# Windowed attention inside an image kernel: 21 passes of three score units instead of 28 of two or three

## The chip, the cores and the metric

The kernel runs on one core of one Trainium2 chip. The metric is the device time of one execution in microseconds. Before the change it is 4560.12 us, the median of three runs (4557.74 to 4571.01).

The core has a matrix engine (PE), a vector engine (DVE), an engine for activations (ACT), a general one (POOL) and one that issues most of the transfers (SP). Each runs its own queue in order; semaphores tie them together. Matrix products land in PSUM[...]; every other tile named here is in SBUF. All data is 32-bit float, and each matmul leaves two records in the trace.

## The reference, cut to what matters

The input is 32 images of 128 channels and 64 x 64 pixels. Each image passes a dynamic 3 x 3 convolution and is then read as 4096 tokens of 128 channels. The tokens are normalised, projected to 16 channels and cut into 55 windows of 144 tokens with a stride of 72, and attention of 4 heads of 4 channels runs inside each window:

```python
win = jnp.transpose(xb[:, idx, :], (0, 1, 3, 2))
flat = win.reshape(Bc * num_w, WIN, D)
qkv = flat @ in_proj_w.T + in_proj_b
...
scores = jnp.einsum('nhqd,nhkd->nhqk', q, k) / np.float32(np.sqrt(HD))
attn = jax.nn.softmax(scores, axis=-1)
o = jnp.einsum('nhqk,nhkd->nhqd', attn, v).transpose(0, 2, 1, 3).reshape(Bc * num_w, WIN, D)
o = o @ out_proj_w.T + out_proj_b
...
recon = jnp.zeros((Bc, Tc, D), xb.dtype).at[:, flat_idx, :].add(o)
```

The result is projected back, added, normalised, and goes through a product with W and a batch norm. A recurrence `y = sigmoid(wx + y @ V.T)` over the 4096 tokens of all images ends the kernel.

## The kernel before, in words

The program has an image stage and, from about 4020 us on, the recurrence (`by_runs`), which has lines of its own and is not touched. It also builds slower branches for other inputs (`images_by_shift`, `by_steps`), which don't run here.

**Who sets the order.** The image stage is a set of Python generators, one for each job and image: `load`, `taps`, `waves`, `conv`, `drain`, `project`, `feed`, `values`, `attend`, `divide0`, `divide1`, `tail`, `last`, and one `setup`. Each yields the engine that its next step needs and the tiles that the step reads and writes. A planner, `Clock`, keeps an account of when each engine and tile is free by a table of costs (`cost`). It takes the step that can start first; between steps that could start at the same time a due time from the table `DUE` decides. A step that yields a fifth value, True, is preferred among these. So the order on each engine is fixed when the program is built, and several images are under way at once. Costs and due times change this order and nothing else. Since every engine is recorded by one helper, all instructions of the stage stand under L242 in the profile; they are told apart by their tiles.

In `cost` a PE step has one of three modes: full (128 x 128 weights), row (32 rows of the array in use, so that four matmuls run side by side on four groups of rows) and col (32 columns, four side by side). A change of mode is charged 0.11.

**Attention of one image.** The windows of an image are handled in `NWG` = 7 blocks `m`, each with `u` = 0 and 1. Four groups of rows `q` work side by side.

- `feed` makes the queries `qs`, the keys `ks`, the last 16 keys of each window spread over eight groups (`kt`), and the values: `Vc` for the first 128 keys and `VT` for the last 16.
- `values` makes for each `s` = 2m + u the masked queries `qe`: POOL multiplies `qs` by the head mask, [128, 4 heads, 144]. Then ACT copies the values into `VE`. There are two buffers of `qe` and of `VE`.
- `attend` runs 14 sets `s` with two passes `hp` each. A pass makes the scores of two heads: four matmuls in row mode with 288 columns each, into the only score tile `sc` (four banks, one for each row group). In the first pass of each block (u = 0, hp = 0) four more matmuls with 144 columns add the scores of the last 16 keys. ACT takes the exponentials of the two heads into `ex` and, in the first pass of a block, those of the extra keys into `ext`, in a second instruction. Then the scores of the next pass may be written. The weighted sums (col mode, 144 columns each) of the pass before follow its scores on PE, into the bank `av`: eight matmuls a pass, and four more with `ext` in each hp = 0. Between passes the planner puts other work of PE, such as the convolution's matmuls with 512 columns (`nm<-u,w`, `nm<-u,h`).
- The bank `av` holds up to three sets (432 columns). DVE copies it to `avs` after the sets 2, 5, 7, 10 and 13. A new group of sets begins with a wait for that copy.
- `divide` divides in two halves (blocks 0 to 3 and 4 to 6) by the sums of the exponentials: transfers to `cd`, a reciprocal, a way through DRAM, a product in `avs`, then a projection in row mode, `sc<-avs,wc`, which uses the same score tile and which DVE adds to `zt`.

Of the kernel before, what the change touches and what calls it, by code (L numbers as in the profile page):

```python
# [8 lines left out]
F32 = mybir.dt.float32  # L9
# [4 lines left out]
P = 128  # L14
# [6 lines left out]
NH = 4  # L21
# [20 lines left out]
    "setup": (0.2, 0.2, 8),  # L42
    "load": (-0.91, 0.63, 29),
    "taps": (0.2, 0.11, 6),
    "waves": (-0.12, 0.52, 26),
    "conv": (-0.43, 1.01, 36),
# [3 lines left out]
    "values": (1.27, 1.15, 28),  # L50
    "attend": (1.24, 1.1, 89),
    "divide0": (1.92, 0.12, 15),
# [6 lines left out]
class Clock:  # L59
# [115 lines left out]
    def cost(self, eng, op, out, ins):  # L175
        n = max(self.width(a) for a in (out, *ins))
        if eng == "PE":
# [7 lines left out]
            if mode != self.mode:  # L185
                c += 0.11
# [71 lines left out]
def hybrid_kernel(  # L258
# [57 lines left out]
    cen = const.tile([P, P], F32, name="cen")  # L316
    nc.vector.tensor_scalar_add(cen, ident, -1.0 / P)
# [36 lines left out]
    bdr = const.tile([P, DK], F32, name="bdr")  # L354
    nc.scalar.dma_start(bdr, b_down.partition_broadcast(P))
    ipr = const.tile([P, 3 * DK], F32, name="ipr")
    nc.scalar.dma_start(ipr, in_proj_b.partition_broadcast(P))
    ipT = const.tile([DK, 3 * DK], F32, name="ipT")
    nc.scalar.dma_start(ipT, in_projT)
    okf = const.tile([P, 1], F32, name="okf")  # L360
    oki = const.tile([P, 1], mybir.dt.int32, name="oki")
    with tc.tile_pool(name="sb1", bufs=1) as sb1, tc.tile_pool(
        name="ps1", bufs=1, space=bass.MemoryType.PSUM
    ) as ps1:
        one_ = sb1.tile([P, P], F32, name="one_")
# [53 lines left out]
    def images(nc):  # L419
# [6 lines left out]
        with ExitStack() as pa:  # L426
# [161 lines left out]
            def load(b):  # L588
# [61 lines left out]
                pl = one.tile([P, P], F32, name="pl")  # L650
# [21 lines left out]
                h = two.tile([P, 9 * P], F32, name="h")  # L672
# [245 lines left out]
            def feed(b):  # L918

                for m0, m1 in ((0, 3), (3, 6), (6, NWG)):  # L920
                    while ("gt", b) not in done or (
                        b and (gone.get(("att", b - 1), 0) <= 4 * m1 if m1 < NWG else ("sets", b - 1) not in done)
                    ):
                        yield
# [61 lines left out]
            exk = kept([P, 2, 4, 2, WIN], "ex")  # L986
            exl = kept([P, 4, WIN], "ext")
            qes = [kept([P, NH, WIN], f"qe{i}") for i in range(2)]

            def values(b):  # L990

                for s in range(2 * NWG):
                    m, u = s // 2, s % 2
                    while ("fed", b, m // 3 * 3) not in done or (
                        gone.get(("att", b), 0) < 2 * s - 1 if s else b and ("sets", b - 1) not in done
                    ):
                        yield
                    o = m * WIN
                    v0 = VEs[s % 2]
                    qe = qes[s % 2]  # L1000
# [7 lines left out]
                    )  # L1008
                    yield "ACT", None, (Vc[:, P * m : P * (m + 1)],), (v0,)
# [8 lines left out]
            def attend(b):  # L1018
# [5 lines left out]
                zt = done["gt", b][0]  # L1024

                def weighted(s, ap, hp, ex, ext):

                    m, u = s // 2, s % 2
                    c0, c1 = group(s)
                    o = slice(WIN * (s - c0), WIN * (s - c0 + 1))  # L1030
                    for h in range(2):
                        for q in range(4):
                            v = NR * (NH * q + 2 * hp + h)
                            nc.tensor.matmul(
                                ap[32 * q : 32 * q + 32, o],
                                VEs[s % 2][:, v : v + 32],
                                ex[:, q, h, :],
                                start=(hp == 0 and h == 0),
                                stop=(hp == 1 and h == 1),
                            )  # L1040
                    if hp == 0:
                        for q in range(4):
                            v = NR * (NQ * m + 2 * q + u)
                            nc.tensor.matmul(
                                ap[32 * q : 32 * q + 32, o],
                                VTf[:, v : v + 32],
                                ext[:, q, :],
                                start=False,
                                stop=False,
                            )  # L1050
                    elif s == c1 - 1:
                        copies.append((av[:, WIN * c0 : WIN * c1], ap[:, 0 : WIN * (c1 - c0)]))

                def group(s):
                    return next(g for g in ((0, 3), (3, 6), (6, 8), (8, 11), (11, 14)) if g[0] <= s < g[1])

                held, copies = None, []
                ap = avp
                exs, ext = exk, exl
                for s in range(2 * NWG):  # L1060
                    m, u = s // 2, s % 2
                    while (b and s == 10 and ("div", b - 1, 1) not in done) or gone.get(("values", b), 0) <= s:
                        yield
                    o = m * WIN
                    qe = qes[s % 2]
                    for hp in range(2):
                        yield "PE", scs, (qe[:, 2 * hp : 2 * hp + 2, :], ks[:, o : o + P], qs[:, o : o + WIN])
                        ps = clock.take("PE", scs)
                        for q in range(4):
                            r = slice(32 * q, 32 * q + 32)  # L1070
                            nc.tensor.matmul(
                                ps[:, q, 0 : 2 * WIN],
                                ks[r, o : o + P],
                                qe[r, 2 * hp : 2 * hp + 2, :],
                                start=True,
                                stop=True,
                            )
# [1064 lines left out]
```

## Time and profile before

| what | value |
|---|---|
| median of 3 runs | 4560.12 us |
| the profiled execution | 4565.91 us |
| its span, first to last instruction | 4564.1 us |
| granted PE clock over the span | 0.968 |
| PE idle before score matmuls (`sc<-qe,ks`) | 103.0 us |
| PE busy in a stretch of 124 us in the middle (2000 to 2124 us) | 120.24 us |

The profile page gives for each engine the busy time and its share of the span. Its groups list, for one kind of instruction, the total and the mean of one, and behind the bar the idle time that the engine had just before these, with what ended it. The waits list who waited for whom, in total microseconds, number of times and the longest. The timeline gives the start, the length and the number of records of merged instructions. A matmul's end is modelled, so that a group's length there can overlap the start of the next; the distance between starts does not.

### The profile page before, as it was taken

What the parts mean: (1) busy time and instruction counts of PE and PEld (TensorE: products, weight loads), DVE (VectorE), ACT (ScalarE), POOL (GpSimd) and SP (SyncE); (2) the same over time, 40 slices, a digit from 0 to 9 for tenths busy, and PEclk for the clock granted to TensorE, in tenths of its full rate; (3) what the DMA queues carried; (4) which work ended last, traced back from release to release, by engine and by line L of the source; (5) the groups of instructions that cost most, each with busy time, mean ns of one, the idle gap of its engine ahead of it and who ended that gap; (6) DMA issues with size and microseconds to landing.
All of it is one profiled execution on the core that took longest, in us unless ns stands there. A gap on an engine that the chain in (4) does not pass through costs nothing. (4 is left out here: it accounts for less than half of the span.)

```text
span 4564.1 us, 102113 instructions
## 1 busy us (share of the span) xinstructions
PE 4165.5 (91%) x41515; PEld 2074.1 (45%) x41515; DVE 3511.6 (77%) x5300; ACT 2465.8 (54%) x3948; POOL 1648.9 (36%) x1652
## 2 busy tenths in 40 slices
PE   5999999999999999999999999999999998589987
PEld 2444444444444444444444444444444444245543
DVE  7778878787787788778787877888778854459884
ACT  1455555545555555555555555555555555357774
POOL 3333333333333333324233333333333412027765
PEclk9999999999999999999999999999999998789998
DMA  3435545454654555555554555455456444459998
GB/s 100 130 108 164 180 158 186 158 174 143 188 179 155 177 177 167 179 162 172 167 185 154 168 176 159 167 179 173 159 163 200 140 168 167 158 222 240 278 268 174
DMA packets 467573, 789.36 MB, mean 173 GB/s; under 512 B 338048, under 2 KB 348304, under 8 KB 434320
## 3 DMA queue, kind: packets, MB, share of 16 engines
q1 hardware_dynamic: 456480, 715.38, 47.4%
q0 software_dynamic: 8704, 67.11, 7.2%
q8 instruction: 332, 5.44, 0.5%
q14 instruction: 153, 1.25, 0.1%
q10 hardware_dynamic: 1904, 0.18, 0.0%
HBM read 499.06 MB, written 276.76 MB: 170 GB/s over the span
## 5 line engine op out<-in xcount | busy, mean ns | idle before, releaser
L242 ACT ACTIVATE ex<-sc 128x1152 f32<-128x1152 f32 x896 | 1013.2, 1131 | 841.7 <-PE sc L242 806.6
L242 POOL TENSOR_TENSOR qe<-qs,mqk 128x576 f32<-128x576 f32 x448 | 605.4, 1354 | 747.5 <-PE sc L242 742.1
L242 PE MATMUL nm<-u,w 128*128 128x512 f32 x1536 | 796.1, 629 | 17.9 <-POOL w L242 16.0
L242 PE MATMUL sc<-qe,ks 32*128 32x288 f32 x7168 | 699.8, 460 | 103.0 <-ACT ext L242 42.4
L242 PE MATMUL av<-ex,VE 128*32 128x144 f32 x14336 | 631.4, 294 | 20.0 <-DVE avs L242 19.9
L242 PEld LDWEIGHTS sc<-qe,ks 32*128 32x128 f32 x7168 | 285.8, 185 | 619.1 <-issue 175.7
L242 PEld LDWEIGHTS av<-ex,VE 128*32 128x32 f32 x14336 | 371.7, 110 | 349.7 <-issue 255.6
L1972 PE MATMUL v<-yw,fVT 128*128 128x254 f32 (+1 forms) x1504 | 436.9, 428 | 34.8 <-ACT yw L1985 25.0
L242 POOL TENSOR_TENSOR u<-frames 128x528 f32<-128x528 f32 x256 | 380.3, 1493 | 185.3 <-PE nm L242 182.7
L1983 ACT ACTIVATE yw<-v,shf 128x254 f32<-128x254 f32 (+1 forms) x752 | 354.6, 474 | 120.6 <-DVE v L1978 48.3
L1978 DVE SCALAR_TENSOR_TENSOR v<-zr,scl,v 128x256 f32<-128x256 f32 (+1 forms) x585 | 347.2, 665 | 90.3 <-PE v L1972 89.8
L242 PE MATMUL nm<-u,h 128*128 128x512 f32 x768 | 397.7, 626 | 3.5 <-DVE frames L242 3.5
L242 PEld LDWEIGHTS nm<-u,w 128*128 128x128 f32 x1536 | 257.3, 191 | 287.6 <-issue 254.4
L1972 PEld LDWEIGHTS v<-yw,fVT 128*128 128x128 f32 x1504 | 241.7, 194 | 243.6 <-ACT yw L1983 194.1
L242 ACT ACTIVATE place<-zt 128x1024 f32<-128x1024 f32 x256 | 262.9, 1053 | 84.8 <-DVE zt L242 66.8
L242 PE MATMUL nm<-zt,fWc 128*128 128x512 f32 x512 | 291.4, 666 | 7.8 <-ACT zt L242 6.9
L1989 POOL COPY zr<-yw 128x256 f32<-128x256 f32 x416 | 256.8, 730 | 85.7 <-ACT yw L1983 85.4
L242 DVE SCALAR_TENSOR_TENSOR u<-u,u 128x528 f32<-128x528 f32 x256 | 244.0, 966 | 49.1 <-POOL u L242 47.6
L242 ACT COPY zt<-nm 128x512 f32<-128x512 f32 x256 | 149.7, 586 | 203.3 <-PE nm L242 197.0
L242 PE MATMUL nm<-place,avg 128*32 128x256 f32 x3072 | 238.3, 391 | 13.5 <-ACT place L242 13.1
L242 POOL TENSOR_TENSOR kt<-ks,mqk 128x384 f32<-128x384 f32 (+1 forms) x96 | 78.3, 815 | 426.2 <-ACT ks L242 381.4
L242 DVE SCALAR_TENSOR_TENSOR zt<-sc,gbk,zt 128x576 f32<-128x576 f32 (+1 forms) x192 | 174.9, 911 | 71.1 <-PE sc L242 70.3
(204 smaller groups left out, 6178.2 us busy)
## 6 DMA issues: line engine op xcount, KB each, us to landing
place<-r_d SPq DMA_DIRECT2D x384, 512.0 KB
place<-in_conv_k_dram SPq DMA_DIRECT2D x128, 576.0 KB
x_d<-frames SPq DMA_DIRECT2D x32, 2112.0 KB
place<-x_d SPq DMA_DIRECT2D x128, 528.0 KB
frames<-in_x_dram SPq DMA_DIRECT2D x128, 512.0 KB
out_dram<-zt SPq DMA_DIRECT2D x64, 1024.0 KB
z_d<-zt SPq DMA_DIRECT2D x64, 1024.0 KB
zr<-z_d SPq DMA_DIRECT2D x26, 2048.0 KB
```

Source lines behind the costliest of these rows:

```text
L242: got = f(*args, **kw)
L1972: nc.tensor.matmul(self.ps[:, :, c], fVT, self.yw[1 - r % 2][:, :, c], start=not whole, stop=True)
L1978: nc.vector.scalar_tensor_tensor(v, z, scl, v, ALU.mult, ALU.add)
L1983: nc.scalar.activation(y[:, :, c], self.ps[:, :, c], AF.Sigmoid, bias=shf)
L1989: nc.gpsimd.tensor_copy(z, y)
```

## The change

Score units are regrouped. A block has nine units of 144 columns: four heads for u = 0, the last 16 keys, and four heads for u = 1. Before, they were made in four passes of 3, 2, 2 and 2 units; after, in three passes of three units each. The middle pass has head 3 of u = 0, the last keys and head 0 of u = 1; these have different weights or queries, so it takes three groups of four matmuls with 144 columns, where the other two passes take four matmuls with 432 columns. One exponential instruction takes all three units. The tile `ex` becomes two tiles of three units, used in turn; `ext` is gone. The weighted sums of a block go to 288 columns of `av`, and DVE copies them to `avs` once a block, seven times an image.

`values` sets a mark of its own behind the queries, and the copy to `VE` waits for a later step of `attend`. `attend` waits for both marks. Gates that count passes are adapted (`feed`).

To make room in SBUF, `cen`, `bdr`, `ipr`, `ipT` and `rep` move into pools or tiles that are free at that time, `pl` becomes a part of `h`, and `cd` has one buffer instead of two. In the planner, leaving full mode is charged 0.19 instead of 0.11, and some due times differ.

```diff
 DUE = {
-    "setup": (0.2, 0.2, 8),
+    "setup": (0.27, 0.02, 8),
...
-    "taps": (0.2, 0.11, 6),
+    "taps": (-0.14, 0.29, 6),
...
-    "conv": (-0.43, 1.01, 36),
+    "conv": (-0.45, 1.09, 36),
...
-    "values": (1.27, 1.15, 28),
-    "attend": (1.24, 1.1, 89),
-    "divide0": (1.92, 0.12, 15),
+    "values": (1.44, 1.24, 28),
+    "attend": (1.24, 1.1, 71),
+    "divide0": (1.88, 0.1, 15),
...
             if mode != self.mode:
-                c += 0.11
+                c += 0.19 if self.mode == "full" else 0.11
...
-                pl = one.tile([P, P], F32, name="pl")
+                h = two.tile([P, 9 * P], F32, name="h")
+                pl = h[:, 0:P]
...
-            exk = kept([P, 2, 4, 2, WIN], "ex")
-            exl = kept([P, 4, WIN], "ext")
+            exs = [kept([P, 4, 3, WIN], f"ex{i}") for i in range(2)]
...
-                        gone.get(("att", b), 0) < 2 * s - 1 if s else b and ("sets", b - 1) not in done
+                        gone.get(("att", b), 0) < 3 * m - 1 + u if m else b and ("sets", b - 1) not in done
...
+                    gone["queries", b] = s + 1
+                    while gone.get(("att", b), 0) < 3 * m + u:
+                        yield
                     yield "ACT", None, (Vc[:, P * m : P * (m + 1)],), (v0,)
...
+                def scores(m, j, ps):
+
+                    o = m * WIN
+                    keys = ks[:, o : o + P]
+                    if j == 1:
+                        units = (keys, qes[0][:, 3]), (kt[:, m], qs[:, o : o + WIN]), (keys, qes[1][:, 0])
+                    else:
+                        units = ((keys, qes[j // 2][:, j // 2 : j // 2 + 3]),)
+                    w = 3 * WIN // len(units)
+                    for i, (k, q) in enumerate(units):
+                        for g in range(4):
+                            r = slice(32 * g, 32 * g + 32)
+                            nc.tensor.matmul(ps[:, g, w * i : w * i + w], k[r], q[r], start=True, stop=True)
+
+                def weighted(m, j, ex):
+
+                    for i in range(3):
+                        if j == 1 and i == 1:
+                            values_of(m, 1, 0, 0, ex[:, :, 1], False, True)
+                        else:
+                            n = 3 * j + i - (3 * j + i > 4)
+                            values_of(m, 0, n // 4, n % 4, ex[:, :, i], n % 4 == 0, n == 7)
+                    if j == 1:
+                        values_of(m, 1, 1, 0, ex[:, :, 1], False, False)
+
+                def values_of(m, extra, u, h, ex, first, last):
+
+                    for g in range(4):
+                        v = NR * (NQ * m + 2 * g + u) if extra else NR * (NH * g + h)
+                        t = VTf if extra else VEs[u]
+                        nc.tensor.matmul(
+                            ap[32 * g : 32 * g + 32, WIN * u : WIN * (u + 1)],
+                            t[:, v : v + 32],
+                            ex[:, g],
+                            start=first,
+                            stop=last,
+                        )
...
-                for s in range(2 * NWG):
-                    m, u = s // 2, s % 2
-                    while (b and s == 10 and ("div", b - 1, 1) not in done) or gone.get(("values", b), 0) <= s:
+                for p in range(3 * NWG):
+                    m, j = p // 3, p % 3
+                    while (
+                        (b and m == 5 and ("div", b - 1, 1) not in done)
+                        or gone.get(("queries", b), 0) <= 2 * m + (j > 0)
+                        or gone.get(("values", b), 0) < 2 * m + j
+                    ):
                         yield
...
+                    scores(m, j, ps)
+                    if held is not None:
+                        if held[1] == 0:
+                            yield "PE", None, (held[2],), (ap,)
+                        else:
+                            yield "PE", None, (held[2],)
+                        weighted(*held)
+                        if held[1] == 2:
+                            copies.append((av[:, 2 * WIN * (m - 1) : 2 * WIN * m], ap[:, 0 : 2 * WIN]))
+                    gone["att", b] = p + 1
+                    ex = exs[(b + p) % 2]
+                    yield "ACT", None, (ps,), (ex,), True
+                    nc.scalar.activation(
+                        ex.rearrange("p q h t -> p q (h t)"), ps[:, :, 0 : 3 * WIN], AF.Exp, scale=HD**-0.5
+                    )
...
-                cdt = two.tile([P, WIN], F32, name="cd")
+                cdt = one.tile([P, WIN], F32, name="cd")
```

## The prediction

> **What bounds it now.** I read the page's busy table first, then the busy time by stretch, to see which engine fills the stage that the change touches; then the waits of that engine, and its timeline, to price it. The busy table of the page:
>
> ```profile
> PE 4165.5 (91%) x41515; PEld 2074.1 (45%) x41515; DVE 3511.6 (77%) x5300; ACT 2465.8 (54%) x3948; POOL 1648.9 (36%) x1652
> ```
>
> Busy time by stretch (columns: length, PE, weight loads, DVE, ACT, POOL, granted clock, DMA share, GB/s):
>
> ```profile
> 1000.00:2000.00 1000.00, 951.46 (x10382) 465.67 (x10380) 791.59 (x1167) 544.23 (x825) 337.30 (x280) 0.98 0.52 167
> 2000.00:3000.00 1000.00, 956.10 (x10458) 468.05 (x10452) 807.59 (x1165) 543.26 (x819) 338.70 (x280) 0.98 0.54 173
> 4020.00:4564.00 544.00, 477.35 (x1620) 264.86 (x1620) 403.19 (x730) 367.64 (x769) 338.22 (x544) 0.94 0.88 240
> ```
>
> The image stage runs to about 4005 us; there PE is busy 95 to 96% of the time and the next engine, DVE, 80%. The last row is the recurrence, which the change leaves alone. The chain that ended last lies wholly in the recurrence, so it doesn't help here: in the image stage PE itself is the chain, and each microsecond taken from PE's order is one off the end, as long as no wait grows.
>
> What it costs PE to do a pass is in its timeline (start, length, group; the 2 records of each matmul are counted in x). I use the distance from one start to the next, because ends are modelled:
>
> ```profile
> 2004.84 0.77 PE L242 MATMUL sc<-qe,ks 32*128 32x288 f32 x8
> 2005.54 0.70 PE L242 MATMUL av<-ex,VE 128*32 128x144 f32 x16
> 2006.06 0.43 PE L242 MATMUL av<-ext,VT 128*32 128x144 f32 x8
> 2006.41 1.13 PE L242 MATMUL nm<-u,w 128*128 128x512 f32 x2
> 2007.47 0.77 PE L242 MATMUL sc<-qe,ks 32*128 32x288 f32 x8
> 2008.06 0.42 PE L242 MATMUL sc<-qs,kt 32*128 32x144 f32 x8
> 2008.41 0.70 PE L242 MATMUL av<-ex,VE 128*32 128x144 f32 x16
> 2009.04 1.99 PE L242 MATMUL nm<-u,w 128*128 128x512 f32 x4
> 2010.95 0.77 PE L242 MATMUL sc<-qe,ks 32*128 32x288 f32 x8
> ...
> 1110.10 1.01 PE L242 MATMUL sc<-avs,wc 17*128 17x432 f32 x8
> 1111.04 1.98 PE L242 MATMUL nm<-u,w 128*128 128x512 f32 x4
> ```
>
> *Full tiles* (128*128): one matmul takes 1.06 to the next start (2006.41 to 2007.47), two take 1.91: 0.86 each and **0.20 a visit**. *Row tiles* (32*128 and 17*128, four side by side): 288 columns take 0.70, 432 take 0.94; so 144 columns cost 0.24, which the extra keys (kt) repeat (0.59 + 0.35 against 0.70), and 0.22 remains **a visit**. *Column tiles* (128*32): 8 matmuls take 0.63 to a full one, and four more, those of VT, lengthen this by 0.24, so streaming is 0.49 and **a visit 0.14**. These steps repeat to a few ns all over the image stage.
>
> **Part 1: 21 passes instead of 28.** Nothing is taken from the work itself: 4,480 score matmuls and 8,960 weighted ones in both kernels, and 9,072 score columns an image in both (28 x 288 + 7 x 144; 21 x 432). What goes are visits. I counted them in the PE order of both built programs, image stage: row tiles are entered 1,078 times before and 840 after, column tiles 1,103 and 928, full tiles 1,043 and 960. So 238 x 0.22 + 175 x 0.14 + 83 x 0.20 = 52 + 24 + 17 = **93 us**. The middle score group of a pass is now three groups of 144 columns; the first of them after a visit begins has no row, but kt's second half follows its first without any extra, so I take 0.22 for it as well (at worst the gain on 224 such passes is 0.1 us less each, 22 us; it could not be better by more than the same). At the granted clock of 0.98 the 93 become 95.
>
> A rule of the Trainium skill speaks against this: TensorEngine Tiling (Array Packing), Performance Considerations, puts the overhead on each matmul, some 60 cycles, whatever its width. By that, with the number of matmuls the same, the change saves nothing: 0 us, and 4560. The row decides against it: four more matmuls in the same mode cost 0.24, which is their columns, and what is left over comes once a visit. The same page says, without a figure, that a change of tiling mode drains TensorE; the visit's 0.14 to 0.22 is what that drain and refill cost here.
>
> **Part 2: the wait for the exponentials.** There is one score tile, so each pass's scores wait for the exponentials of the pass before, and PE must have other work meanwhile. PE's waits:
>
> ```profile
> PE sc L242 <- ACT ext L242: 46.0, 43, 3.0
> PE sc L242 <- ACT ex L242: 35.2, 63, 3.0
> PE av L242 <- DVE avs L242: 19.9, 11, 4.8
> PE sc L242 <- POOL qe L242: 17.0, 24, 3.7
> ```
>
> The rows of ACT and of the copies:
>
> ```profile
> L242 ACT ACTIVATE ex<-sc 128x1152 f32<-128x1152 f32 x896 | 1013.2, 1131 | 841.7 <-PE sc L242 806.6 <-DVE cp L242 19.3 <-DVE bnmv L242 8.6
> L242 ACT ACTIVATE ext<-sc 128x576 f32<-128x576 f32 x224 | 144.5, 645 | 0.0
> L242 DVE COPY avs<-av 128x432 f32<-128x432 f32 x128 | 77.0, 601 | 93.8 <-PE av L242 93.1
> L242 DVE COPY avs<-av 128x288 f32<-128x288 f32 x32 | 14.4, 451 | 33.9 <-PE av L242 33.9
> ```
>
> From 576 and 1152 elements (645 and 1131 ns) a start of 159 ns and 0.844 ns an element: 1728 elements take 1.62 us. From the start of its scores to the earliest next scores a plain pass needs 0.70 + 0.20 (ACT's start behind the scores, 2005.74 in the trace) + 1.13 + 0.06 = about 2.1 us; the pass with the extra keys 0.94 + 0.20 + 1.13 + 0.65 = about 2.85 (two exponentials); every pass after, 0.94 + 0.20 + 1.62 + 0.06 = 2.8. So the longest wait is not longer, while every pass brings 12 or 16 weighted matmuls instead of 8 or 12 to fill it. Before, the pass with the extra keys had 0.94 + 0.63 of its own and lacked 1.3 us, more than one 512-column matmul's 1.06; after, each has 0.94 + 0.87 or more and lacks at most 1.0, which one such matmul covers. I then walked the PE order of both programs with the steps above and summed what falls short between two passes: before, 133 passes lack 84 us (the trace has 46.0 + 35.2 on ACT and part of 17.0 on POOL, so the walk can be trusted); after, 94 passes lack 49. That is **35 us** less. ACT's work falls from 1,158 to 672 x 1.62 = 1,087 us, unseen at 54% busy.
>
> **Part 3: copies per block.** Five copies an image become seven of 288 columns: from 128 x 0.601 + 32 x 0.451 = 91 to 224 x 0.451 = 101 us of DVE, hidden behind PE. The weighted matmuls of a new block wait for the copy, with at least the next scores and a filler (0.94 + 1.06) in between, where before it was 0.70 + about 0.8. So the 19.9 us may rise with 224 chances for 160 (+8) or go (-20); I take 0. SBUF moves (cen, cd, pl, the small loads) and the setup's due times act once, or reuse a tile whose last reader is a whole phase past; no DMA is added, SP's transfers are the same in number. 0 us, up to 10 either way. The query multiplies on POOL (1.35 us each) get two whole passes' time, about 4.6 us; before, about 3.5. The copy into VE now waits for a step of attend of its own. In the built order of ACT it stands between the exponentials of two passes, so the later ones are queued behind it, and behind these PE's next scores; but there ACT waits for PE anyway (806.6 us of idle in the row of ex), and the copy is 0.24 us: nothing, or at worst its 448 x 0.24 x the share of passes that are short (94 of 672), 15 us, which the 10 to 35 below take in.
>
> **Part 4: due times and a dearer tile change** only reorder; their visits and lacks are already in the counts. What is late next is DVE: 98.7 us an image of some 123 before (its mean over six stretches of one image each), of some 119 after, 83%. PE already waits for DVE 39.3 us at the divided outputs and 20 at the convolution's; I charge 10 us more (0 to 35).
>
> **Sum.** -95 - 35 + 10 = -120 on the profiled execution of 4565.9 (span 4564.1 and 1.8 around it): 4446. That run lies 5.8 above the median, so 4560 - 120 = **4440**.
>
> **Rivals.** (a) *Given back*: the visits go, but DVE and the order around it take up the slack, as PE's waits for ACT don't shrink and those for DVE grow by 35: -95 + 35 = -60, 4500. For it: DVE at 80% and in order; against: the walk's fit to the waits of before. (b) *More*: all the avs wait and most of the ACT wait go, and fewer holes keep the clock up (0.98 in the middle, 3,780 x 0.02 = 75 us lost, a third back): -95 - 60 - 20 - 5 = -180, 4380. (c) *Slower*: ACT is in order, and a copy of 0.59 us (nm to zt) or 0.24 (VE) that stands before the exponentials delays the only score tile; with 1.62 us to follow, the filler then falls short. It decides from 130 / 672 = 0.19 us a pass upward; at 0.25 a pass, 168 us, the time is 4600. Against: only 94 passes are short by count. The same page of the skill, under PSUM Bottleneck, warns that emptying PSUM becomes the limit after tiling, and wants two engines for it; here ACT alone does it, yet 21 x 2.8 = 59 us an image is half of the period, so by the trace it doesn't bind. (d) That it doesn't do what it says: the order shows 672 passes of 1728 elements; nothing is left for it but chance.
>
> **How the numbers follow.** Forecast 0.60 (own range 4410 to 4470); (a) 0.25; (b) 0.09; (c) 0.04; (d), or no change, 0.02. The range reaches to (a)'s 4500 less a little and below the forecast's end, since the widest sums of the unknowns are -50 and -165: 4402 to 4492. A change under 0.3% can't be told from none here. Faster 0.94, same 0.02, slower 0.04.
>
> **What would show it.** PE busy in the image stage down by some 95 us with idle lower by about 30; score groups of 432 columns at 0.94 to the next start; the middle group near 0.95; ACT's row for 1728 elements at 1.62; waits of sc for ACT near 50 us. It is wrong if the middle group costs over 1.05, if the waits for ACT pass 100, or if those for DVE grow by more than 35.

## The result, and the profile after

The changed kernel takes **4505.22 us**, the median of four runs (4492.03 to 4507.87); the kernel before, in four runs on the same chip, takes 4565.57. The ratio is 0.9861 (95% interval 0.9831 to 0.9891). The change makes the kernel faster by 1.4%, half of the forecast 120 us; 4505 lies 13 us above the range of 4402 to 4492.

The profiled execution takes 4507.87 us, its span is 4506.1, and the clock granted over it 0.958 (0.968 before). First the busy table of the page after, one line:

```profile
PE 4099.9 (91%) x41515; PEld 2055.8 (46%) x41515; DVE 3562.1 (79%) x5364; ACT 2407.2 (53%) x3500; POOL 1680.8 (37%) x1652
```

Then the busy time by stretch (columns: length, PE, weight loads, DVE, ACT, POOL, granted clock, DMA share, GB/s):

```profile
1000.00:2000.00 1000.00, 956.30 (x10650) 471.45 (x10648) 834.26 (x1199) 535.23 (x712) 354.74 (x285) 0.97 0.55 174
2000.00:3000.00 1000.00, 946.33 (x10524) 468.95 (x10522) 835.74 (x1212) 539.67 (x727) 356.11 (x291) 0.97 0.54 172
3962.00:4506.00 544.00, 478.27 (x1620) 264.76 (x1618) 401.64 (x723) 366.00 (x769) 338.60 (x544) 0.94 0.88 239
```

The recurrence (last row) is what it was. In the image stage more matmul records fit in 1000 us, but PE isn't less idle, and the clock fell from 0.98 to 0.97. The steps that were priced beforehand are all there. The timeline of two passes after (start, length, group; the last one is cut short):

```profile
955.67 0.53 PE L242 MATMUL sc<-qe,ks 32*128 32x144 f32 x8
956.02 0.42 PE L242 MATMUL sc<-qs,kt 32*128 32x144 f32 x8
956.26 0.42 PE L242 MATMUL sc<-qe,ks 32*128 32x144 f32 x8
956.62 0.94 PE L242 MATMUL av<-ex,VE 128*32 128x144 f32 x24
957.49 0.38 PE L242 MATMUL nm<-cv,grp 128*128 128x1 f32 x2
...
959.29 1.01 PE L242 MATMUL sc<-qe,ks 32*128 32x432 f32 x8
960.23 0.45 PE L242 MATMUL av<-ex,VE 128*32 128x144 f32 x8
```

A score group of 432 columns takes 0.94 to the next start, the middle group 0.35 + 0.24 + 0.36 = 0.95, twelve weighted matmuls 0.87. So do the rows of the exponentials and of the copies (1611 ns against 1.62 forecast, 100.6 us against 101):

```profile
L242 ACT ACTIVATE ex<-sc 128x1728 f32<-128x1728 f32 x672 | 1082.5, 1611 | 869.0 <-PE sc L242 854.6 <-DVE u L242 7.0 <-PE av L242 5.2
L242 DVE COPY avs<-av 128x288 f32<-128x288 f32 x224 | 100.6, 449 | 190.7 <-PE av L242 189.6
```

What is different is whom PE waits for. The waits after:

```profile
PE sc L242 <- DVE zt L242: 90.2, 47, 4.7
PE nm L242 <- DVE h L242: 52.6, 20, 3.5
PE sc L242 <- ACT ex L242: 28.2, 54, 1.2
...
PE sc L242 <- ACT VE L242: 12.2, 17, 0.8
PE sc L242 <- DVE avs L242: 10.6, 8, 5.6
...
PE sc L242 <- POOL qe L242: 2.6, 1, 2.6
PE av L242 <- DVE avs L242: 2.0, 4, 0.7
```

and before, the two that grew (the scaled plane had a tile of its own, `pl`):

```profile
PE sc L242 <- DVE zt L242: 39.3, 27, 4.8
...
PE nm L242 <- DVE pl L242: 18.0, 8, 2.9
```

The wait for the exponentials of the extra keys (46.0) is gone, that for `ex` fell from 35.2 to 28.2, for `qe` from 17.0 to 2.6, for the copies into `avs` from 19.9 to 2.0. In their place PE waits for DVE: 51 us more where it waits for `zt`, 35 more where the logits product (`nm<-fcwT`) waits for the scaled plane.

I then added up, over the image stage (from the span's start to the first matmul of the recurrence), PE's idle time by the engine that released it, and the time that the clock took away (half of every period granted at half speed). "Work" is the count of PE's visits and columns in the built order, priced as in the prediction; what is left over in the sum is 13 us before and -6 after, so sums of this kind are good to some 20 us.

| image stage, us | before | after | difference |
|---|---|---|---|
| end of the stage | 4021.6 | 3961.5 | -60 |
| PE's work by count | 3563 | 3471 | -92 |
| lost to the half-speed clock | 112 | 156 | +44 |
| PE idle | 333 | 340 | +7 |
| of it for DVE | 170 | 231 | +61 |
| for ACT | 121 | 74 | -48 |
| for POOL | 34 | 28 | -6 |

The visits came as counted. The missing 60 us are idle time that did not fall by 25 but rose by 7, and a clock that was taken as given and lost 44. Together these are 76; the other 16 lie within what the sum leaves over.

**The first new hole.** The timeline after, around one logits product (the brackets give the idle time before and who ended it; only the lines of three engines that matter are kept):

```profile
961.10 1.31 POOL L242 TENSOR_TENSOR kt<-ks,mqk 128x384 f32<-128x384 f32 x1
...
961.63 0.79 DVE L242 TENSOR_TENSOR gl<-gr 128x1 f32<-128x1 f32 x1
...
962.36 1.30 POOL L242 TENSOR_TENSOR u<-frames 128x528 f32<-128x528 f32 x1
962.45 1.23 DVE L242 SCALAR_TENSOR_TENSOR gl<-gv,gl 128x1 f32<-128x1 f32 x1
963.63 1.14 POOL L242 TENSOR_TENSOR qe<-qs,mqk 128x576 f32<-128x576 f32 x1
963.72 0.15 DVE L242 TENSOR_SCALAR gl<-gl 128x1 f32<-128x1 f32 x1
963.90 0.88 DVE L242 TENSOR_TENSOR gr<-gr,gl 128x1 f32<-128x1 f32 x1
...
965.26 0.36 PE L242 MATMUL nm<-fcwT,h 128*128 128x4 f32 x2 [2.97 <-DVE h L242]
...
966.48 1.82 PE L242 MATMUL sc<-qe,ks 32*128 32x432 f32 x8
```

Three steps on a single column take 0.79, 1.23 and 0.88 us; each ends where the GpSimd product beside it ends (962.41, 963.66, 964.77). The step at 963.72, which has only one input in SBUF, takes 0.15 beside the same product. PE waits 2.97 us for the chain, of which the three steps have 2.4 from standing beside GpSimd, and the scores that follow are 1.82 long where those at 959.29 are 1.01: the clock has dropped to half. DVE is not idle before the step that writes the scaled plane, in either trace, so the plane's move into `h` isn't what delays it. Of the 96 such two-input steps (32 images, three each) 31 took more than 0.25 us before and 57 after, and every one of these ended within 0.2 us of the end of a GpSimd instruction. The tile's own rows (shortest/median/longest ns) before:

```profile
L242 DVE TENSOR_TENSOR gl<-gr x32: 147/160/1283, 28.5 to 3582.0; 128x1 f32<-128x1 f32 x32
L242 DVE SCALAR_TENSOR_TENSOR gl<-gv,gl x32: 159/160/1280, 28.7 to 3583.4; 128x1 f32<-128x1 f32 x32
```

and after:

```profile
L242 DVE TENSOR_TENSOR gl<-gr x32: 147/491/1148, 28.8 to 3548.7; 128x1 f32<-128x1 f32 x32
L242 DVE SCALAR_TENSOR_TENSOR gl<-gv,gl x32: 158/1165/1253, 29.0 to 3549.5; 128x1 f32<-128x1 f32 x32
```

The Trainium skill has the rule behind it (SBUF — State Buffer, Who interferes with whom): a DVE instruction with both inputs in SBUF and a GpSimd instruction that reads SBUF exclude each other for the whole instruction. The rows agree, for steps of a single column too. The kernel's planner counts this exclusion only for steps wider than one column, so it places these chains as if GpSimd were not there.

**The second.** The timeline after, at a divided output:

```profile
981.02 1.01 PE L242 MATMUL sc<-avs,wc 17*128 17x432 f32 x8
...
984.38 0.45 DVE L242 COPY avs<-av 128x288 f32<-128x288 f32 x1
...
984.52 1.01 PE L242 MATMUL sc<-avs,wc 17*128 17x432 f32 x8 [2.48 <-DVE zt L242]
984.75 1.21 DVE L242 TENSOR_TENSOR zt<-zt,place 128x1024 f32<-128x1024 f32 x1
986.00 1.29 DVE L242 BATCH_NORM_STATS2 st<-zt 128x6 f32<-128x512 f32 x2
987.20 1.10 DVE L242 SCALAR_TENSOR_TENSOR zt<-sc,gbk,zt 128x864 f32<-128x864 f32 x1
988.33 0.97 DVE L242 TENSOR_TENSOR zt<-zt,sc 128x432 f32<-128x432 f32 x2
...
989.36 0.86 PE L242 MATMUL sc<-qe,ks 32*128 32x144 f32 x8 [3.83 <-DVE zt L242]
...
990.00 0.70 PE L242 MATMUL sc<-qs,kt 32*128 32x144 f32 x8
990.48 0.70 PE L242 MATMUL sc<-qe,ks 32*128 32x144 f32 x8
```

The score tile is held until DVE has added the product to `zt`. Before it gets there it does a copy, a product of the third normalisation and two statistics, 2.8 us. PE stands for 3.83 us. Of the groups of 144 columns behind it, the second takes 0.48 to the next start (990.00 to 990.48); at full clock it took 0.24 (956.02 to 956.26).

### The profile page after: what moved, and what is told of

It reads as the page before. It is cut to its first block, busy times and chain, and to the rows that moved or that the text cites. A ratio compares the mean times of both kernels' runs of the same rounds, so it can differ in the third digit from the quotient of the medians.

```text
span 4506.1 us, 101240 instructions
## 1 busy us (share of the span) xinstructions
PE 4099.9 (91%) x41515; PEld 2055.8 (46%) x41515; DVE 3562.1 (79%) x5364; ACT 2407.2 (53%) x3500; POOL 1680.8 (37%) x1652
## 5 line engine op out<-in xcount | busy, mean ns | idle before, releaser
L242 ACT ACTIVATE ex<-sc 128x1728 f32<-128x1728 f32 x672 | 1082.5, 1611 | 869.0 <-PE sc L242 854.6
L242 PE MATMUL nm<-u,w 128*128 128x512 f32 x1536 | 779.9, 625 | 24.8 <-POOL w L242 24.6
L242 PE MATMUL sc<-qe,ks 32*128 32x432 f32 (+1 forms) x7168 | 689.0, 455 | 83.9 <-DVE zt L242 39.2
L242 PEld LDWEIGHTS av<-ex,VE 128*32 128x32 f32 x14336 | 396.5, 111 | 309.7 <-issue 250.8
L242 POOL TENSOR_TENSOR u<-frames 128x528 f32<-128x528 f32 x256 | 411.1, 1614 | 60.1 <-PE nm L242 57.3
L242 DVE COPY avs<-av 128x288 f32<-128x288 f32 x224 | 100.6, 449 | 190.7 <-PE av L242 189.6
L242 PE MATMUL sc<-avs,wc 17*128 17x288 f32 (+1 forms) x1536 | 174.8, 516 | 69.8 <-DVE zt L242 51.0
```

Source lines behind the costliest of these rows:

```text
L242: got = f(*args, **kw)
```

## The experiments

Throughout, "exact order" means that the planner was told (`clock.note`) that the old instruction had run, so that no other instruction moved. Times are medians; ratios are to runs of the kernel before on the same chip, with 95% intervals.

### The change taken apart

The regrouped passes with the old due times and the old flat price of a tile change (one of the due times is shown):

```diff
...
-    "conv": (-0.45, 1.09, 36),
+    "conv": (-0.43, 1.01, 36),
...
-                c += 0.19 if self.mode == "full" else 0.11
+                c += 0.11
```

> The three-unit passes with the due times of before and the flat 0.11 for a tile change. By count its PE order has 2,568 changes of tile mode against 2,728 in the changed kernel, worth some 28 us of PE work less, and its passes lack 96 us of other work instead of 49. Theory 'order' (the due times and the dearer change make PE stand behind DVE; the regrouping alone keeps its gain): near 4460, PE's waits for DVE in the image stage back near those of before (about 110 us). Theory 'DVE' (with shorter PE work DVE falls behind in any order): 4500 or above, waits for DVE over 150 us again, or moved to the exponentials.

The reverse, the old passes with the new due times and price (in `attend` 89 steps are kept):

> The passes of before with the new due times and the 0.19. Changes of tile mode by count 3,205, as many as before (3,224); lack of other work 53 us against 84. Theory 'order': slower than before, 4580 to 4630, since the waits behind DVE (logits product, divided outputs) come along with the due times. Theory 'DVE': 4535 to 4565, waits for DVE as before, because PE's work is as long as before.

And the changed kernel with only the price put back to 0.11:

> The changed kernel with 0.11 for every tile change in the planner's account, due times as changed. Changes of tile mode by count 2,614; lack of other work 81 us against 49. If the corrected account earns something, this is slower than the changed kernel by 10 to 30 us (4515 to 4535); if its order is one of many alike, it lies within 15 us of 4505, with the lumps of wait elsewhere.

Measured: the passes alone **4591.46** (ratio 1.0040, 1.0025 to 1.0055), the due times and price on the old passes **4582.44** (1.0023, 1.0014 to 1.0032), the change with the flat price **4592.68** (1.0047, 1.0032 to 1.0061). No part gains; each is a little slower than before. The passes do save visits in the first and the third (the count of PE's work in the first is 3442, 121 less than before), but in the first PE is idle for 435 us, 102 more than before, and loses 170 to the clock, 58 more. So the gain belongs to the passes only together with the order.

Is the order after one among many? The due time of the convolution moved by 0.01, in the changed kernel and in the one before:

```diff
-    "conv": (-0.45, 1.09, 36),
+    "conv": (-0.44, 1.09, 36),
```

> The changed kernel with one due time moved by a hundredth (conv from -0.45 to -0.44): an order like it that nobody has picked. If 4505 is what the regrouping with the corrected account is worth, 4495 to 4520. If it is one picked order among many, with the others where the old due times and the flat charge were, 4540 to 4600; then most of the spread lies in PE's waits for ACT and DVE, not in its visits.

> The kernel before with the convolution's due time moved by 0.01. If before is itself a picked order, as the changed kernel is, its neighbour is slower: 4590 to 4640. If the old passes have the slack for it, 4560 to 4575. The first would mean that the change is worth its 95 us between orders that were not picked.

Measured: **4570.44** for the changed kernel (1.0005, 0.9996 to 1.0015): the whole gain is gone. **4601.7** for the kernel before (1.0085, 1.0069 to 1.0102). In both kernels the one neighbour that was tried is slower, by 65 and 36 us, so each looks like an order picked among many. The stage shows what the other orders have in common; the last two columns are PE's waits for `zt` before a matmul into the score tile and for the scaled plane before the logits product:

| planned with the old account | passes | time | work | idle | clock | `zt` | logits |
|---|---|---|---|---|---|---|---|
| before, picked | old | 4565.6 | 3563 | 333 | 112 | 39 | 18 |
| new due times | old | 4582.4 | 3561 | 340 | 139 | 62 | 30 |
| conv by 0.01 | old | 4601.7 | 3563 | 352 | 132 | 60 | 22 |
| after, picked | new | 4505.2 | 3471 | 340 | 156 | 90 | 53 |
| old due times | new | 4591.5 | 3442 | 435 | 170 | 85 | 27 |
| flat price | new | 4592.7 | 3451 | 421 | 163 | 78 | 32 |
| conv by 0.01 | new | 4570.4 | 3449 | 396 | 163 | 76 | 27 |

In the three orders with the new passes that were not picked, PE works about 115 us less than in the two with the old passes that were not (3447 for 3562 on the mean), is idle for 71 more and loses 30 more to the clock. Nearly all is given back. The two new holes differ here. The wait for `zt` is longer with the new passes in every one of these orders. The wait at the logits product is long in the picked order alone: in the others it is what orders with the old passes have, and 28, 28 and 22 of the 96 small steps are late, not 57.

### Is it the load of DVE?

DVE is busier after (3562 us for 3512). If that is the limit, less work must help. In the exact order of each kernel, the third normalisation's statistics read 8 columns of 512 instead of all (what is left out is the rest of the sums). Their row falls from 164.6 to 30.3 us, by 134 rather than the 154 expected; DVE's whole busy time falls by 118 us after and 135 before.

```diff
-  nc.vector.bn_stats(st[:, 2 * i + j, :], z[:, BLK * j : BLK * (j + 1)])
+  clock.nc.vector.bn_stats(st[:, 2 * i + j, :], z[:, BLK * j : BLK * j + 8])
+  clock.note("DVE", "bn_stats", ...)
```

> The changed kernel in exactly its order, but the statistics of the third normalisation (256 instructions of DVE, 0.685 us each) read 8 columns instead of 512, so that the batch norm's scale and shift are those of a sample: 256 x 0.6 = 154 us of DVE work less, with nothing else moved. Theory 'DVE' (PE stands because DVE is behind): 4420 to 4465, PE's waits for DVE fall by more than half and the granted clock rises. Theory 'order' (PE's order has nothing to put in those places, DVE is not late by load but by what it is given first): 4490 to 4505.

> The kernel before in exactly its order, with the same shortening of the third normalisation's statistics as in the changed kernel (8 columns of 512, 154 us of DVE less). Control: if relief of DVE is worth as much here as in the changed kernel (18 us), the changed kernel is no more bound by DVE's load than the one before: about 4550. If DVE's load had become the limit only by the change, nothing moves here: 4563 to 4572.

Measured: **4487.01** (ratio 0.9822, 0.9795 to 0.9848) for the changed kernel, 18 us less than it had; before, in a single run, **4558.35** beside 4571.84. The 18 is rough, since the intervals of the two ratios overlap. It lies just under the 4490 to 4505 expected if the load doesn't count, and far from the 4420 to 4465 if it does. 134 us of DVE are worth about 18 and 13 us, in the one kernel as in the other, so the load as such is not what changed. PE's idle time for DVE stays at 233 us in the first (231 after); what fell is the clock's loss, from 156 to 121.

A planning step made finer, so that the divide's additions can come between the product and its two statistics (three steps in place of one):

```diff
...
   nc.vector.tensor_mul(z, z, w[:, 0:QT])
-  for j in range(2):
-      nc.vector.bn_stats(...)
+  return [lambda j=j: nc.vector.bn_stats(...) for j in range(2)]
```

> The changed kernel; in the third normalisation the product and the two statistics (1.2 + 0.7 + 0.7 us of DVE) are three steps for the planner instead of one, so that the additions of divide can come between. Nothing is left out; the order is new. If the holes at the score tile come from such long steps standing ahead of these additions, PE's waits for DVE there fall from 90 to below 60 us and the time to 4460 to 4490. If the waits are only placed by the order as a whole, they stay at 80 to 100 and the time lies anywhere from 4500 to 4600, as with the other new orders.

Measured: **4584.93** (1.0037, 1.0024 to 1.0049), idle 407 of which 234 for DVE, clock 178. PE's wait for `zt` is 83 us, where less than 60 was expected if the long step is the cause. This doesn't settle it: the whole order moved, and one like the others that were not picked came out.

### The two holes by themselves

The logits product in the exact order, reading the identity instead of the scaled plane, so that PE has nothing to wait for (the taps then don't depend on the plane):

```diff
-  nc.tensor.matmul(lg_ps[:, 0:NK], pl, fcwT, start=True, stop=True)
+  clock.nc.tensor.matmul(lg_ps[:, 0:NK], ident, fcwT, start=True, stop=True)
+  clock.note("PE", "matmul", (lg_ps[:, 0:NK], pl, fcwT), {})
```

> The changed kernel in exactly its order, but the product of the logits reads the identity instead of the tile that DVE makes last, so the mixing coefficients are others and PE doesn't wait there. Theory 'places' (PE's order puts the logits product, and the divided outputs, where the small steps of DVE can't have been done, and each hole brings a half-speed window): the 52.6 us of wait go and most of the 35.8 us that half-speed windows cost behind them, so 4420 to 4455. Rival 'moved on' (all that follows needs DVE as well, so the next instruction waits instead): 4480 to 4505, with other waits for DVE up by about 50.

> Control to the logits product that doesn't wait: the same edit in the kernel before, in its order. There PE waits 18 us at this place and 12 us of half-speed windows follow, against 52.6 and 35.8 in the changed kernel. If those holes are what the change gave back, the gain here is a third of the 33 us there: 5 to 15 us (ratio 0.997 to 0.999). If the edit helps for another reason, about 30 us here too (ratio 0.993).

Measured: **4474.89** after (0.9785, 0.9766 to 0.9804), which is 30 us below the changed kernel, less than the 50 to 85 expected from the wait and the clock behind it: PE's idle time for ACT rises by some 20 us, so part of the wait moved on. **4569.45** before (0.9996, 0.9984 to 1.0008), nothing. This hole is the changed kernel's own, and by the table above it is its order's rather than the passes'.

The divide's additions on 8 columns instead of 288 or 432 (the rest of the sums is left out), in the exact order:

```diff
-  zs, ps[:, 0:2, 0:n], gbk, zs, ALU.add, ALU.add
+  zs[:, :, 0:8], ps[:, 0:2, 0:8], gbk, zs[:, :, 0:8], ALU.add, ALU.add
...
+  clock.nc.vector.tensor_add(zs[:, :, 0:8], zs[:, :, 0:8], ps[:, 2:4, 0:8])
...
```

> The changed kernel in exactly its order, but DVE adds only 8 columns of each product of divide to the output, so the score tile is held by DVE for about 0.4 us instead of 1.6 to 2.2. Theory 'places': PE's waits for DVE at the score tile (90 us) fall by more than half and the half-speed windows behind them (58 us lost) with them, so 4400 to 4440. Rival 'queue' (PE waits for what stands ahead of these adds on DVE, not for the adds): the waits stay over 60 us and the time lies at 4470 to 4500, the 320 us of DVE work saved giving about as much as the 154 us of the short statistics.

> Control to the short additions of divide: the same edit in the kernel before, in its order. There PE waits 40 us for DVE at the score tile and 22 us of half-speed windows follow, against 90 and 58. If the score tile's holes behind divide grew with the change, the gain here is half or less of the 66 us there: 20 to 40 us (ratio 0.991 to 0.996). If it is the 320 us of DVE work that counts, the gain is the same 60 to 70 us (ratio 0.985).

Measured: **4438.62** after (0.9706, 0.9680 to 0.9733), 67 us below the changed kernel; **4514.45** before (0.9873, 0.9854 to 0.9892), some 55 us below its own time on that chip (4569.91), more than the 20 to 40 expected. DVE's busy time falls by 253 and 265 us. Most of what this relief brings is thus common to both kernels; about 12 us, or 13 by the ratios, are new. PE's idle time for DVE in the changed kernel falls from 231 to 187.

Both reliefs at once, in both kernels:

> The changed kernel's exact order with both reliefs at once: the logits product reads the identity instead of the scaled plane (which leaves out the dependence of the taps on the plane), and VectorE adds only 8 columns of each of the divide's products. Alone they gave 30 and 67 us. If the two holes are separate, the sum holds: 4400 to 4415. If one hole only moves to the other's place, 4430 to 4440. In either case a step that removes both would bring the forecast of 4440 back, and the excess over it lies in these two holes and the clock that follows them.

> The exact order of the kernel before with both reliefs: the logits product reads the identity (which leaves out the taps' dependence on the plane) and VectorE adds only 8 columns of each of the divide's products. With the same two reliefs the changed kernel has 4405.9. If the changed kernel lost half of its gain in these two places and the clock behind them, the distance comes out near the forecast's 120: this gives 4505 to 4525, a distance of 100 to 120. If VectorE's work is simply the next limit in both kernels, the relief brings as much here as there, 160 us down to 4465, and the distance stays at 60.

Measured: **4405.89** after (0.9659, 0.9641 to 0.9677) and **4520.19** before (0.9882, 0.9866 to 0.9899). The two reliefs add up in the changed kernel (30 + 67 = 97; 99 measured). And with both taken from both kernels the change is worth 114 us by the medians, 102 by the ratios. The stage of the two says how: ends 3854.4 and 3976.9, work 3471 and 3563, clock 106 and 112, idle 280 and 295. That is close to the forecast: the visits, some less idle time (15 us, for a forecast 25), and about the same clock.

### The rule that the planner lacks

The planner's rule for DVE behind GpSimd, extended to two inputs of a single column and to wide operations with a scalar from SBUF to SBUF:

```diff
-  both = sum(1 for a in ins if self.sbuf(a) and self.width(a) > 1) > 1
+  w = max((self.width(a) for a in ins), default=0)
+  both = sum(1 for a in ins if self.sbuf(a) and self.width(a) == w) > 1
+  both = both or (op.startswith("tensor_scalar") and w >= 64 and self.sbuf(out) and self.sbuf(ins[0]))
```

First in the changed kernel, then in the kernel before, then in the changed kernel with the convolution's due time moved by 0.01:

> The changed kernel with an account in which DVE's one-column steps with two tile inputs and its copies by a scalar stand behind POOL's products, as the trace shows them to (a 0.15 us step took 0.79 to 1.23 beside POOL). By count its order is new. Theory 'mispriced' (the logits product is put too early because these steps are charged too little): PE's wait for h falls below 20 us, and the time below the changed kernel's, 4450 to 4490. If other orders are simply worse than the tuned one, 4520 to 4600, with the logits wait low all the same.

> The passes of before with its own due times; only the planner's rule changes: one-column steps of VectorE with two inputs in SBUF, and wide copies with a scalar, are counted as standing behind GpSimd's products. If that rule was wrong for the old order too, VectorE's holes in PE (170 us before) fall and the time with them, to 4500 to 4550. If the rule matters only where passes of three leave VectorE late, the order is merely another draw: 4560 to 4600, with more holes than before, as in the other orders that were not fitted.

> The order with the small steps counted (4512.93), and the convolution's due time moved by 0.01, the same step that cost the changed kernel its whole gain (4505 to 4570). If counting the small steps is what gains, this stays at 4500 to 4535, with VectorE's holes near 193 us. If that order was a lucky one among many, this goes to 4560 to 4595 with holes of 220 to 240 us.

Measured: **4512.93** (0.9868, 0.9850 to 0.9885), **4593.89** (1.0063, 1.0046 to 1.0081) and **4538.46** (0.9940, 0.9923 to 0.9957). With the new passes the rule comes out where the fitted order is, though the due times are not fitted to it; its neighbour is 26 us slower, just outside the 4500 to 4535 expected, and still faster than before: 4538 where the neighbour under the old rule had 4570. With the old passes the rule brings nothing (4594, among 4582 and 4602 of the other old orders). The logits product waits less, as the waits of the first show, though PE then waits more for ACT:

```profile
PE sc L244 <- ACT ex L244: 81.6, 107, 2.2
PE sc L244 <- DVE zt L244: 55.5, 38, 5.8
...
PE nm L244 <- DVE h L244: 15.6, 9, 2.9
```

DVE's share of the idle time is 193 us and the clock's loss 121, against 231 and 156 after. The small steps are short again (35 of 96 over 0.25 us). They need not be what gains: in the neighbour 22 of them are late under the old rule and 19 under the new, 32 us apart in time. The rule has two parts, small steps and wide operations with a scalar, and they were not tried one by one.

Last, due times fitted to this rule. It is a complete kernel:

```diff
...
-    "taps": (-0.14, 0.29, 6),
-    "waves": (-0.12, 0.52, 26),
+    "taps": (-0.09, 0.29, 6),
+    "waves": (-0.12, 0.49, 26),
...
-    "divide0": (1.88, 0.1, 15),
-    "divide1": (2.21, 0.02, 11),
+    "divide0": (1.88, 0.17, 15),
+    "divide1": (2.14, 0.02, 11),
```

> A complete kernel: the passes of three, the planner's rule that counts small VectorE steps behind GpSimd, and due times fitted anew to that rule (setup 0.02 to 0.04, taps -0.14 to -0.09, waves 0.52 to 0.49, divide0 0.1 to 0.17, divide1 2.21 to 2.14; the rest as in the changed kernel). Its PE order has 2,591 changes of tile mode, 137 fewer than the changed kernel's. If the lost half lies in holes that a better informed order can close, it falls below both: 4440 to 4490, VectorE's holes under 200 us, the clock's loss at 100 to 125. If an order's rank in the planner's account tells nothing of the chip's time, it lands where its neighbours do, 4510 to 4540.

Measured: **4443.18** (4437.65 to 4449.77; ratio 0.9714, 0.9698 to 0.9731), below both kernels: 2.9% faster than before, and 62 us faster than the changed one by the medians, 67 by the ratios. Its stage ends at 3903.5, with 3447 of work, 333 idle (175 for DVE, 121 for ACT), and 115 lost to the clock: idle time and clock as before the change, and the visits gone, 116 us of them, more than the 93 of the changed kernel. That it stands at the forecast's number is luck: the sum is another. The passes of before were not fitted to this rule, so how much of the 2.9% is owed to the new passes isn't shown. Its waits, in the same lines as above:

```profile
PE sc L244 <- ACT ex L244: 62.0, 98, 1.7
PE sc L244 <- DVE zt L244: 49.0, 35, 5.7
...
PE nm L244 <- DVE h L244: 9.6, 8, 2.9
```

## Why the prediction was half wrong

**Part 1 held.** The visits fell to the counts, each step has its forecast length, the middle group included (0.95), and the work by count fell by 92 for 93. An overhead on each matmul, which would have made it 0, doesn't show in the same rows, whose matmuls have 144 columns or more.

**Part 2 held in its own term and beyond it.** PE's idle time for ACT fell by 48 for 35, and the waits for `qe` and of the weighted sums for `avs` fell by a further 14 and 18. But this belongs to the picked order, not to the passes: in the three orders with new passes that were not picked PE is idle for ACT for 155, 148 and 133 us, more than the 121 before. The walk of PE's order was right for the order that it was made for (49 us counted, 40 waited for ACT before score matmuls) and near for the first two of these (96 and 81 counted, 106 and 97 waited).

**Part 3 held.** Copies of 100.6 us; no DMA more; the copy into `VE` is waited for 12.2 us, within what was set aside.

**Part 4 is the step that failed.** "I charge 10 us more (0 to 35)" for DVE; it was 61. The charge was taken from DVE's busy share and from two waits, 39.3 and 20 us, of the 170 that PE had for DVE. DVE's busy share is not the cause: 134 us less work brought about 18. What counts is where single DVE steps stand: 35 us more at the logits product, 51 more at `zt`, 25 less elsewhere. I had read the busy rows of DVE and not its short steps: the rows `gl` and `gr` of before already show a longest of 1283 ns for a step whose median is 160. Which GpSimd products would stand beside them in the changed kernel's planned order I didn't ask.

**And one term was missing.** "At the granted clock of 0.98 the 93 become 95" treats the clock as a constant. It isn't one: it follows the holes. It lost 112 us before and 156 after. Both holes bring it down: with each half-speed period put down to the longest hole in the 3.41 us ahead of it, those behind a wait at the logits product cost 12 us before and 36 after, those behind a `sc<-avs,wc` that waited for `zt` 22 and 48. The planner, which I had, accounts for this: `turn` and `pace` double the length of PE's steps after a window of 3.413 us in which PE was used for less than half. I put the change of the clock at nothing without asking it.

**The range was drawn too narrow.** It is said to come from sums of -50 and -165; from 4560 these give 4510 and 4395, not 4492 and 4402.

Of the 60 us missing, the reliefs in both kernels settle the larger part: they take 99 us from the changed kernel and 51 from the one before by the medians, 92 and 54 by the ratios, so 38 to 48 sit in the two places and the clock behind them. The rest, 12 to 22, isn't assigned.

Rival (a), 4500, named nearly the right number and half of the mechanism: waits for DVE grew, by 61 where it said 35; but the waits for ACT did shrink, and the clock, which it had not, took what that gave. Rival (b), more, expected that fewer holes would keep the clock up; the holes didn't become fewer, and the clock fell. Rival (c), 4600, is near what the passes give in orders that were not picked (4570 to 4593), where the waits for ACT do grow, but not as one delay of 0.19 us a pass: DVE and the clock have their shares in it. What would have shown the forecast wrong was written down as "if those for DVE grow by more than 35", and that is what happened.

What stays open: why orders with passes of three have more holes at all, above all longer waits for `zt`. That fewer, longer passes leave fewer places to put other work is plausible and was not tried. It isn't a limit of the passes, as the fitted kernel shows.

## What to carry to other kernels

When a change regroups work under a planner, its gain has two parts, the work that goes and the order that comes out; compare several orders of each version (a due time moved by a hundredth is enough) before believing either, here 65 and 36 us apart. A step that is short by its median can still be the wait: look at the longest of a row beside its median, and ask which other engine was running then. And price an idle hole with what follows it: here a stretch of 3.4 us in which PE stood for about half cost it half its speed in the next.

## What the runs showed of the hardware

- The clock fell to half after stretches in which PE was idle for about half of the time, not only after empty ones: over the 3.41 us before each half-speed period after the change, PE was idle for at least 0.45 of it (median 0.69 in 46 periods). The periods begin and end on one grid of 3.41 us. Of the full-speed stretches of this grid (from 100 us on), 44 of the 46 that were idle for 0.45 or more were followed by half speed, and none of the 997 with less; before the change, 30 of 40 and 3 of 1048. The Trainium skill (TensorE: Matmul & The Clock Gate, The HAM clock gate) lets the clock drop after an idle window of about 3.4 us; here the longest single hole in such a stretch was between 0.9 and 3.4 us, with short matmuls around it. The periods last multiples of 3.41 us, as its window says.
- DVE steps on one column with two inputs in SBUF wait for the end of a GpSimd product: 0.16 us alone, up to 1.3 beside one; a step with one such input (`gl<-gl`) keeps its 0.15, in all 19 cases beside GpSimd work after the change.
